# Second cross-attention and feed-forward as one hand-ordered stretch, with softmax inverses and keys and values by way of DRAM

## The chip, the cores and the metric

The kernel runs on one core of one Trainium2 chip. The metric is the device time of one execution in microseconds. A core has five engines that this document speaks of: TensorE (PE in the profile; its weight loads are the row PEld), VectorE (DVE), ScalarE (ACT), GpSimd (POOL) and SyncE (SP), which here only issues DMAs. Each engine works through its own list of instructions in order and waits on semaphores for what others produce. Data moves between DRAM and the on-chip memory (SBUF) by 16 DMA engines; matmul results land in eight banks of PSUM.

## The reference

Two transformer blocks over `x` of shape (8, 512, 256), all in float32. The first block is a self-attention with per-head normed queries and keys, a cross-attention to 64 context tokens, and a gated feed-forward. The second block, cut to what the change touches:

```
cross_in = adaln(x, cond, ...)              # layernorm over 256, then scale and shift per batch
ctx_n    = ln(context)                      # (8, 64, 192)
x = attn(cross_in, ctx_n, ca_wq, ca_wkv, ca_wo, ca_bo) + x
ffn_in = adaln(x, cond, ...)
h = gelu(ffn_in @ ff_w1 + ff_b1)            # 256 -> 1024
x = h @ ff_w2 + ff_b2 + x

attn: q = rope(heads(xq @ wq)); k = rope(heads(ctx @ wk)); v = heads(ctx @ wv)   # 16 heads of 64
      a = softmax(q k^T / 8)                # over the 64 context tokens
      out = (a v) @ wo + bo
```

## The kernel before, in words

All of `x` stays in SBUF as eight tiles of 128 partitions x 4 x 256 (`xs[b]`), and every stage updates it in place. The stages follow one another: block 0 (until about 835 us), block 1's self-attention (the pool `ph4`, until about 1906), its cross-attention (`ph5`, until about 2279) and its feed-forward (`ph6`).

The order of instructions is set in two ways. Block 0 and the self-attention stand under `tc.manual_schedule`, which keeps TensorE, VectorE, ScalarE and POOL in the order in which the program emits them; SP's DMAs are ordered by a planner. The pools `ph5` and `ph6` stand outside it, and the planner orders all engines, starting from `run_blocks`, which places a step some blocks before or after the scores it belongs to.

Self-attention (`slots`) runs over 128 slots: 8 batches x 4 groups of 4 heads x 4 tiles of keys. Each slot makes scores, exponentials, and the products with the values of the slot before. Row sums of the exponentials are made by POOL and VectorE into tiles `sm` (L907, L911) and by TensorE (`sums`). They go by way of DRAM: ScalarE copies them to `den`, a DMA writes them to `den_d` (L929), another reads them back spread over 128 partitions (L935), VectorE takes reciprocals (L939), a DMA writes them to `rec_d` (L941), and two DMAs load them as `rb`, two rows spread over 64 partitions each (L950). POOL multiplies the attention output `oT` by `rb` (L955), and `project_out` makes the output rows of two 128-row tiles, which VectorE adds to `x` (L396). At the end of the stage `cross_values` makes the values of the cross-attention for all batches, eight pairs of heads one after another, and writes them to the DRAM tile `v_d`; the keys `k_d` were written by `keys1` during block 0, with the same layout.

The cross-attention (`batch5`) does for each batch:

- `norm`: layernorm of `x` (L187 to L191, with a power on POOL, L179), eight transposes on TensorE (L366), scale and shift on ScalarE (L367), and the addition of the output bias on POOL (L380).
- `context`: load the keys and values of the batch from `k_d` and `v_d` into one of two buffers, block-diagonally for a pair of heads.
- `outer`: values times output weights for two pairs, so that the weighted sum and the output projection are one matmul per pair (`vw`, L1063).
- `queries(p)`: the query of pair p, then the rope: three VectorE multiplications (L720, L723) and a POOL addition (L724).
- `score`: the scores of two pairs and their exponential on ScalarE (`p`, L1079).
- `sums`: row sums by 16 matmul instructions, VectorE's reciprocal of all 128x512 of them straight from PSUM (L1091), a write to DRAM by four DMAs (L1095), and for each two pairs two loads into `rb`, 64 partitions at a time (L1101), followed by a multiplication of `p` by `rb` on POOL or VectorE in turn (L1104).
- `project_out` with `vw`: the output rows, added to `x`.

The feed-forward makes for each batch four pairs of up-projections with GELU (L1155), prepares the next batch's normed input, projects down and stores the batch. PSUM is shared by `bank_s` (two tiles of two banks, scores), `bank_o` and `bank_d` (one bank each) and `bank_x` (two banks). `bank_x` also takes `bank_d` in turn during block 0, but not after it.

Of the kernel before, what the change touches and what calls it, by code (L numbers as in the profile page):

```python
# [78 lines left out]
def fast_path(ctx: ExitStack, tc: tile.TileContext, a: dict, out: bass.AP):  # L79
# [8 lines left out]
    turns = [0]  # L88
# [10 lines left out]
    def bank_x():  # L99
        if turns:  # L100
            turns[0] += 1
            if turns[0] % 3 == 0:
                return bank_d()
        return psum.tile([P, 512], F32, tag="X", name="ps_X", bufs=2)

# [268 lines left out]

    def normed_T(pool, x, b, eps, am, bm, bufs=2):
        return transposed(pool, normed(pool, b, eps), b, am, bm, bufs)
# [335 lines left out]
    k_d = dram.tile([B, P, NPAIR, T], F32, name="k_d", bufs=1)  # L712
    v_d = dram.tile([B, P, NPAIR, T], F32, name="v_d", bufs=1)
# [23 lines left out]
    def keys1(p):  # L737
        ps = bank_x()
        for k in range(2):
            mm(ps, kv1["w"][:, k, p * P : (p + 1) * P], ctxzT[:, k, :], k == 0, k == 1)  # L740
        q = kv1["pool"].tile([P, N], F32, tag="q", name="q")
        rope_pair(kv1["pool"], ps.rearrange("p (j n) -> p j n", j=B), kv1["rope_c"][:, None, :], kv1["rope_s2"][:, None, :],
                  [P, B, T], q.rearrange("p (j n) -> p j n", j=B))
        nc.sync.dma_start(k_d[:, :, p, :].rearrange("b r t -> r b t"), q.rearrange("p (b t) -> p b t", b=B))
# [56 lines left out]
    turns.clear()  # L801
# [9 lines left out]
    def load_kb(b):  # L811
        for i in range(4):
            r = slice(32 * i, 32 * i + 32)
            nc.sync.dma_start(kvs[b % 2][0][r, :, i % 2, :], k_d[b, r])

    def load_vb(b):
        for e in range(2):
            r = slice(64 * e, 64 * e + 64)
            nc.sync.dma_start(kvs[b % 2][1][r, :, e, :], v_d[b, r])
# [5 lines left out]
    def cross_values(wk, p):  # L825
# [3 lines left out]
        v = wk.tile([P, N], F32, tag="k0", name="v")  # L829
        nc.scalar.copy(v, ps)  # L830
        nc.sync.dma_start(v_d[:, :, p, :].rearrange("b r t -> r b t"), v.rearrange("p (b t) -> p b t", b=B))


    with tc.tile_pool(name="ph4", bufs=2) as wk:
        NG = H // 4
        kb, vb = kv_first()
        steps, mid = {}, {}
# [164 lines left out]
        def slots():  # L1002
            n = B * NG * NT
            for i in range(-2, n + 1):
# [9 lines left out]
                if i == n - 5:  # L1014
                    cross_weights()
            sums, sums_back, inverse, inverse_back, scaled, out_tiles = todo[-1][-1]
# [6 lines left out]
            load_vb(0)  # L1023
            for qp in range(2):
# [5 lines left out]
    w_co, w_cq, rope_s2 = cross["o"], cross["q"], cross["s"]  # L1030


    with tc.tile_pool(name="ph5", bufs=2) as wk:
        kvs.append(tuple(wk.tile([P, NPAIR, 2, T], F32, name=n, bufs=1) for n in ("kb", "vb")))
        for z in kvs[1]:
            nc.gpsimd.memset(z, 0.0)

        w_f1 = load_w("ff_w1", 1)
        w_f2 = load_w("ff_w2", 3)
        blocks = []  # L1040

        def batch5(b):
            s = {}

            def norm():
                s["hT"] = transposed((nk, wk)[b % 2], normed(nk, b, EPS1), b, a1, b1, 1)
                add_row(b, row("cabo"))

            def context():
                s["kb"], s["vb"] = kvs[b % 2]  # L1050
                if b:
                    load_kb(b)
                    load_vb(b)

            def outer(pp):

                if pp == 0:
                    s["vw"] = wk.tile([P, NPAIR, D], F32, tag="vw", name="vw", bufs=3)
                ps = bank_x()
                for i in range(2):  # L1060
                    p = 2 * pp + i
                    mm(ps[:, i * D : (i + 1) * D], s["vb"][:, p, :, :].rearrange("p e k -> p (e k)"), w_co[:, p, :])
                nc.scalar.copy(s["vw"][:, 2 * pp : 2 * pp + 2, :], ps.rearrange("p (i d) -> p i d", i=2))  # L1063

            def queries(p):
                ps = bank_x()
                for k in range(2):
                    mm(ps, w_cq[:, k, p * P : (p + 1) * P], s["hT"][:, k, :], k == 0, k == 1)
                s[p] = q = wk.tile([P, N], F32, tag="q", name="q", bufs=6)
                rope_pair(wk, ps[:, None, :], rope_c[:, None, :], rope_s2[:, None, :], [P, 1, N], q[:, None, :])  # L1070

            def block(pp):
                def score():
                    ps = bank_s()
                    for i in range(2):
                        p = 2 * pp + i
                        mm(ps[:, i, :], s["kb"][:, p, :, :].rearrange("p e k -> p (e k)"), s[p])
                    s["p", pp] = wk.tile([P, 2, N], F32, tag="p", name="p", bufs=8)
                    nc.scalar.activation(s["p", pp], ps, AF.Exp, scale=HD1 ** -0.5)  # L1079

                return Block([score], [])

            def sums():

                d = bank_d()
                for i in range(2):
                    for j in range(4):
                        p = 4 * i + j
                        mm(d[32 * j : 32 * j + 32, :], sel3[:, i, :], s["p", p // 2][:, p % 2, :], i == 0, i == 1)
                rec = wk.tile([P, N], F32, tag="rec", name="rec", bufs=1)  # L1090
                nc.vector.reciprocal(rec, d)  # L1091
                rd = dram.tile([NPAIR, 2, N], F32, tag="rec5", name="rec5")
                for i in range(2):
                    for e in range(2):
                        nc.sync.dma_start(rd[4 * i : 4 * i + 4, e, :],  # L1095
                                          rec.rearrange("(j r) n -> j r n", j=4)[:, 2 * i + e, :])
                check(rec)
                for pp in range(4):
                    rb = wk.tile([P, 2, N], F32, tag="rb", name="rb")
                    for e in range(2):  # L1100
                        nc.sync.dma_start(rb[64 * e : 64 * e + 64, :, :],  # L1101
                                          rd[2 * pp : 2 * pp + 2, e, :][None].to_broadcast([64, 2, N]))
                    eng = (nc.gpsimd, nc.vector)[pp % 2]
                    eng.tensor_tensor(s["p", pp], s["p", pp], rb, ALU.mult)  # L1104

            for pp in range(4):
                bl = block(pp)
                if pp == 0:
                    bl.before += [(5, norm), (4, context)]
                bl.before.append((1, lambda pp=pp: outer(pp)))  # L1110
                bl.before += [(2, lambda pp=pp: queries(2 * pp)), (2, lambda pp=pp: queries(2 * pp + 1))]
                blocks.append(bl)
            bl.after.append((0, sums))
            for qp in range(2):
                bl.after.append((2 + qp, lambda qp=qp: project_out(qp, lambda k: s["p", k // 2][:, k % 2, :], s["vw"], 8,
                                                                  add_to(b))))

        for b in range(B):
            batch5(b)
# [907 lines left out]
```

## Time and profile before

| | us |
|---|---|
| three timed runs, median (range) | 2523.02 (2521.21 to 2523.74) |
| the profiled run: its time | 2522.38 |
| its span, first to last instruction | 2520.5 |

Busy time by stage, in us, from the profiled run:

| stage | length | TensorE | VectorE | ScalarE | POOL | granted TensorE clock | DMA share |
|---|---|---|---|---|---|---|---|
| block 0 (0 to 835) | 835 | 804.7 | 387.7 | 398.0 | 242.8 | 0.98 | 0.12 |
| self-attention of block 1 (to 1906) | 1071 | 1048.7 | 441.4 | 354.6 | 435.6 | 0.99 | 0.08 |
| cross-attention (to 2279) | 373 | 349.0 | 236.1 | 62.8 | 153.1 | 0.99 | 0.24 |
| feed-forward (to the end) | 241.5 | 234.6 | 30.0 | 56.0 | 19.5 | 1.00 | 0.05 |

How to read it: an engine's busy share is an average over the stage; what a stage costs is decided by the engine that others wait for, and by the waits that stand on that engine. The granted clock is the share of full speed at which TensorE was allowed to run. The DMA share is the mean over the 16 DMA engines, so 0.125 can be all of them an eighth of the time or two of them all of the time. Lines of the profile that give a start, a length and in square brackets an idle time name after the arrow what ended that idle time. A float32 matmul shows as two instructions.

### The profile page before, as it was taken

The page shows a single profiled execution, that of the slowest core. Times are in us where ns is not written, and L with a number is a line of the kernel's source. Part 1 is how long each engine was busy: PE and PEld are TensorE (multiplying, and loading weights), DVE is VectorE, ACT ScalarE, POOL GpSimd, SP SyncE. Part 2 cuts the span into 40 slices and gives each one's busy share as a digit, 9 for nine tenths or more (in the row PEclk, how much of TensorE's full clock was granted, in tenths as well). Part 3 has the DMA queues.
Part 4 walks back from the last instruction along what each step waited for, and adds up shares of the span by engine and source line. Part 5 has one row for each costly group of instructions (what it writes and reads, how often), then busy time and mean ns, then how long its engine had stood idle before and what let it go on. Part 6 is the DMA issues. An engine that isn't in the chain of part 4 may idle for free.

```text
span 2520.5 us, 27970 instructions
## 1 busy us (share of the span) xinstructions
PE 2437.0 (97%) x10938; PEld 1152.9 (46%) x10938; DVE 1095.1 (43%) x2039; ACT 871.3 (35%) x1099; POOL 850.9 (34%) x521
## 2 busy tenths in 40 slices
PE   8999999999999899999999999999989999999999
PEld 3333443443445533434343434343435456556665
DVE  4555435435435334343444434445326765652000
ACT  3555546545542133242424243333232111112221
POOL 3453222322300035353535353536324434431000
PEclk9999999999999999999999999999999999999999
DMA  5130000000002000000000000000131321320000
GB/s 180 35 95 9 16 17 10 16 11 12 12 11 88 0 4 28 18 18 18 19 18 18 18 18 18 18 18 18 51 92 40 79 49 42 76 68 9 17 17 26
DMA packets 91084, 83.76 MB, mean 33 GB/s; under 512 B 51104, under 2 KB 67424, under 8 KB 90936
## 3 DMA queue, kind: packets, MB, share of 16 engines
q1 hardware_dynamic: 90388, 81.34, 11.0%
q8 instruction: 88, 1.44, 0.2%
q10 hardware_dynamic: 556, 0.55, 0.1%
q14 instruction: 52, 0.43, 0.1%
HBM read 72.09 MB, written 9.77 MB: 32 GB/s over the span
## 4 chain that ended last, share of the span: by engine, by line
PE 87%; DVE 4%; DMA 3%; issue 2%; POOL 2%; ACT 2%; SPq 0%; DVEq 0%; POOLq 0%; ACTq 0%
PE ps_X L107 42%; PE ps_S L107 22%; PE ps_D L107 11%; PE ps_O L107 9%; PE ps_X L366 1%; DMA rb<-rec_d 1%; DVE t L723 1%; ACT p L505 1%; POOL q L724 1%; DMA rb<-rec 1%; DVE t L720 1%; DVE st L187 1%; PE ps_X L485 0%; POOL p L1104 0%; PE ps_X L527 0%
## 5 line engine op out<-in xcount | busy, mean ns | idle before, releaser
L107 PE MATMUL ps_S<-q,k 32*128 32x512 f32 (+1 forms) x3072 | 432.5, 628 | 7.0 <-ACT p L505 3.4
L892 ACT ACTIVATE p<-ps_S 128x1024 f32<-128x1024 f32 x256 | 248.4, 1022 | 526.6 <-PE ps_S L107 519.1
L505 ACT ACTIVATE p<-ps_S 128x1024 f32<-128x1024 f32 x256 | 248.2, 1022 | 259.7 <-PE ps_S L107 258.8
L107 PEld LDWEIGHTS ps_S<-q,k 32*128 32x128 f32 (+1 forms) x3072 | 160.6, 185 | 245.7 <-issue 136.4
L871 DVE TENSOR_TENSOR t<-ps_X,rope_c 128x512 f32<-128x512 f32 x126 | 87.1, 691 | 341.0 <-PE ps_X L107 341.0
L911 DVE TENSOR_TENSOR sm<-sm,p 128x1024 f32<-128x1024 f32 x128 | 192.3, 1546 | 55.6 <-ACT p L892 54.3
L396 DVE TENSOR_TENSOR x<-ps_X,x 128x512 f32<-128x512 f32 x48 | 33.2, 692 | 342.6 <-PE ps_X L107 342.6
L874 POOL TENSOR_TENSOR q<-t 128x512 f32<-128x512 f32 x32 | 40.7, 1273 | 384.2 <-DVE t L872 384.2
L107 PE MATMUL ps_X<-hT,w 128*128 128x512 f32 x344 | 160.6, 601 | 1.6 <-DVE t L678 1.1
L907 POOL TENSOR_TENSOR sm<-p 128x1024 f32<-128x1024 f32 x64 | 149.2, 2353 | 32.5 <-ACT p L892 32.5
L724 POOL TENSOR_TENSOR q<-t,t 128x512 f32<-128x512 f32 x72 | 97.2, 1353 | 159.0 <-DVE t L723 151.3
L107 PE MATMUL ps_O<-p,h 128*32 128x512 f32 x1024 | 138.1, 612 | 0.5 <-ACT oT L518 0.5
L107 PE MATMUL ps_O<-p,v 128*64 128x512 f32 x512 | 138.0, 617 | 0.0
L107 PE MATMUL ps_D<-p,v 128*64 128x512 f32 x512 | 131.6, 592 | 1.1 <-ACT p L892 1.1
L179 POOL TENSOR_TENSOR rstd<-rstd,mhalf 128x4 f32<-128x4 f32 x49 | 49.6, 1015 | 241.4 <-DVE rstd L178 239.3
L107 PE MATMUL ps_X<-vw,p 128*128 128x256 f32 x512 | 119.2, 389 | 10.9 <-DVE p L1104 9.8
L107 PE MATMUL ps_X<-w_sa_wo,oT 128*128 128x256 f32 x512 | 118.0, 389 | 11.2 <-DVE oT L955 6.4
L380 POOL TENSOR_TENSOR x<-x,rows 128x1024 f32<-128x1024 f32 x24 | 56.5, 2354 | 196.9 <-DVE z L191 195.4
L107 PE MATMUL ps_X<-hT,w_sa_wq 128*128 128x512 f32 x256 | 115.9, 595 | 4.2 <-ACT hT L367 4.2
L107 PE MATMUL ps_X<-w_sa_wv,hT 128*128 128x512 f32 x256 | 118.0, 604 | 0.0
L107 PE MATMUL ps_S<-hT,w_ff_w 128*128 128x512 f32 x256 | 117.9, 604 | 0.1
L107 PE MATMUL ps_X<-hT,w_ca_wq 128*128 128x512 f32 x256 | 117.3, 598 | 0.7 <-DVE t L723 0.7
(219 smaller groups left out, 3546.4 us busy)
## 6 DMA issues: line engine op xcount, KB each, us to landing
rb<-rec SPq DMA_DIRECT2D x80, 256.0 KB
rb<-rec_d SPq DMA_DIRECT2D x62, 256.0 KB
x<-in_x_dram SPq DMA_DIRECT2D x8, 512.0 KB
out_dram<-x SPq DMA_DIRECT2D x8, 512.0 KB
bc<-modd SPq DMA_DIRECT2D x8, 384.0 KB
gate<-modd SPq DMA_DIRECT2D x16, 128.0 KB
k_d<-q SPq DMA_DIRECT2D x8, 256.0 KB
v_d<-v SPq DMA_DIRECT2D x8, 256.0 KB
```

The costliest lines, as they stand in the source:

```text
L107: nc.tensor.matmul(o, lhsT, rhs, start=start, stop=stop)
L179: nc.gpsimd.tensor_tensor(r[:, :n], r[:, :n], mhalf[:, :n], ALU.pow)
L187: nc.vector.bn_stats(st[:, t, :], src[:, t, :])
L380: nc.gpsimd.tensor_tensor(xs[b], xs[b], r[:, None, :].to_broadcast([P, NT, D]), ALU.add)
L396: nc.vector.tensor_tensor(x, ps, x, ALU.add)
L505: nc.scalar.activation(pr[u], pss[u], AF.Exp, scale=HD0 ** -0.5)
L724: nc.gpsimd.tensor_tensor(dst, t1, t2, ALU.add)
L871: nc.vector.tensor_tensor(c, ps, rope_c, ALU.mult)
L874: nc.gpsimd.tensor_tensor(r[0], ec, os, ALU.subtract)
L892: nc.scalar.activation(pr, pss[u], AF.Exp, scale=HD1 ** -0.5)
L907: nc.gpsimd.tensor_tensor(sm, s["p", g, 0, u], s["p", g, 1, u], ALU.add)
L911: nc.vector.tensor_tensor(s["sm", g, u], s["sm", g, u], s["p", g, t, u], ALU.add)
```

## The change

- The cross-attention and the feed-forward become one pool (`ph5`) in one `manual_schedule`, in the order in which `cross()` and `feed_forward()` emit their steps. A batch of the cross-attention is eight steps of a pair of heads. The queries run three pairs ahead of the scores. The inverses, multiplications and output tiles of a batch stand within the next batch's steps; those of the last batch stand within the feed-forward.
- The row sums go to DRAM first (four writes, `den5`), come back spread over 128 partitions, VectorE takes reciprocals of 64 columns, one DMA writes them (`rec5`), and each pair's `rb` is loaded by one DMA as two rows spread over 64 partitions each. POOL and VectorE multiply one pair each in turn.
- `k_d` and `v_d` are laid out by pairs, so that what `keys1` and `cross_values` write is contiguous in each partition; the reads follow.
- The norm and bias addition of batch 0 are emitted in self-attention's slot 123 and its transposes before the last output tiles; values are copied to tiles of two names in turn.
- `bank_x` takes `bank_d` and `bank_o` in turn as well during the new stretch.
- A batch is stored in two halves; the hidden layer has one buffer.

```
-    k_d = dram.tile([B, P, NPAIR, T], F32, name="k_d", bufs=1)
-    v_d = dram.tile([B, P, NPAIR, T], F32, name="v_d", bufs=1)
+    k_d = dram.tile([P, NPAIR, B, T], F32, name="k_d", bufs=1)
+    v_d = dram.tile([P, NPAIR, B, T], F32, name="v_d", bufs=1)
...
-        nc.sync.dma_start(k_d[:, :, p, :].rearrange("b r t -> r b t"), q.rearrange("p (b t) -> p b t", b=B))
+        nc.sync.dma_start(k_d[:, p], q.rearrange("p (b t) -> p b t", b=B))
...
-            nc.sync.dma_start(kvs[b % 2][0][r, :, i % 2, :], k_d[b, r])
+            nc.sync.dma_start(kvs[b % 2][0][r, :, i % 2, :], k_d[r, :, b, :])
...
-        v = wk.tile([P, N], F32, tag="k0", name="v")
+        v = wk.tile([P, N], F32, tag=f"k{p % 2}", name="v")
         nc.scalar.copy(v, ps)
-        nc.sync.dma_start(v_d[:, :, p, :].rearrange("b r t -> r b t"), v.rearrange("p (b t) -> p b t", b=B))
+        nc.sync.dma_start(v_d[:, p], v.rearrange("p (b t) -> p b t", b=B))
...
                 if i == n - 5:
                     cross_weights()
+                    first_rows.append(normed(nk, 0, EPS1))
+                    add_row(0, row("cabo"))
...
             scaled(NG - 1, [nc.gpsimd, nc.vector])
             load_vb(0)
+            first_rows.append(transposed(nk, first_rows[0], 0, a1, b1, 1))
             for qp in range(2):
                 out_tiles(qp)
...
+    extra.extend([bank_d, bank_o])
     with tc.tile_pool(name="ph5", bufs=2) as wk:
...
+        def sums(b):
+            s = ss[b]
+            d = bank_x()
...
+            den = wk.tile([P, N], F32, tag="den", name="den", bufs=1)
+            nc.scalar.copy(den, d)
+            dd = dram.tile([NPAIR, 2, N], F32, tag="den5", name="den5")
+            for i in range(2):
+                for e in range(2):
+                    nc.sync.dma_start(dd[4 * i : 4 * i + 4, e, :], den.rearrange("(j r) n -> j r n", j=4)[:, 2 * i + e, :])
+            s["rec"] = rec = wk.tile([P, H * N // P], F32, tag="rec", name="rec", bufs=1)
+            nc.sync.dma_start(rec, flat(dd))
+
+        def inverse(b):
+            s = ss[b]
+            rec = s["rec"]
+            nc.vector.reciprocal(rec, rec)
+            rd = dram.tile([NPAIR, 2, N], F32, tag="rec5", name="rec5")
+            nc.sync.dma_start(flat(rd), rec)
+            check(rec)
+            s["rd"] = rd
+
+        def scaled(b):
+            s = ss[b]
+            for p in range(NPAIR):
+                rb = wk.tile([P, N], F32, tag="rb", name="rb", bufs=4)
+                nc.sync.dma_start(rb, s["rd"][p, :, None, :].to_broadcast([2, 64, N]))
+                pr = s["p", p // 2][:, p % 2, :]
+                (nc.gpsimd, nc.vector)[p % 2].tensor_tensor(pr, pr, rb, ALU.mult)
+
+        def out_tile(b, t, lhsT, w):
+            s = ss[b]
+            if t % 2 == 0:
+                s["ps"] = bank_x()
+            project_tile(s["ps"], t % 2, lhsT, w, 8, t)
+            if t % 2:
+                add_to(b)(t // 2, s["ps"].rearrange("p (j d) -> p j d", j=2))
...
+        def cross():
+            LEAD = 3
+            for n in range(LEAD):
+                queries(n)
+                if n == 0:
+                    rows_(1)
+            for z in kvs[1]:
+                nc.gpsimd.memset(z, 0.0)
+            for b in range(B):
+                for j in range(NPAIR):
+                    if j % 2 == 0:
+                        score(b, j // 2)
+                    if j == 6 and b:
+                        cross_out(b - 1, 2)
+                    queries(NPAIR * b + j + LEAD)
+                    if j < 2:
+                        outer(b, 2 * j)
+                        outer(b, 2 * j + 1)
+                    if b:
+                        if j == 1:
+                            inverse(b - 1)
+                        if j == 3:
+                            scaled(b - 1)
+                        if j in (4, 5, 7):
+                            cross_out(b - 1, j - 4)
+                    if j == 2 and b + 1 < B:
+                        load_kb(b + 1)
+                        load_vb(b + 1)
+                    if j == 4:
+                        turn(b + 1)
+                    if j == 5:
+                        rows_(b + 2)
+                    if j == 7:
+                        sums(b)
+
+        def feed_forward():
+            good = None
+            for b in range(B):
+                for ff in range(4):
+                    up(b, ff)
+                    if b == 0 and ff == 1:
+                        inverse(B - 1)
+                    if b == 0 and ff == 3:
+                        scaled(B - 1)
+                if b == 0:
+                    for t in range(4):
+                        cross_out(B - 1, t)
+                turn(B + b + 1)
+                for t in range(4):
+                    down(b, t)
+                    if t == 1:
+                        rows_(B + b + 2)
...
+        with tc.manual_schedule(engines={ENG.PE, ENG.DVE, ENG.Activation, ENG.Pool}):
+            cross()
+            return feed_forward()
```

`rows_` is the layernorm and bias addition of a batch, `turn` its transposes with scale and shift, `cross_out(b, t)` the output tile t of the cross-attention, `up` and `down` the two halves of the feed-forward.

## The prediction

> **What bounds the kernel now.** I read the page's first part, then busy time by stage, then the chain and TensorE's waits in the last two stages, and last the queue rows and DMA share around the loads called rb.
>
> ```profile
> PE 2437.0 (97%) x10938; PEld 1152.9 (46%) x10938; DVE 1095.1 (43%) x2039; ACT 871.3 (35%) x1099; POOL 850.9 (34%) x521
> ...
> 1906.00:2279.00 373.00, 348.97 (x1217) 201.54 (x1215) 236.11 (x354) 62.77 (x80) 153.07 (x98) 0.99 0.24 59
> 2279.00:2520.50 241.50, 234.59 (x836) 149.20 (x834) 29.99 (x66) 56.00 (x81) 19.50 (x10) 1.00 0.05 18
> ```
>
> TensorE (first number after each length) is the bound, also in the second cross-attention (1906 to 2279) and the feed-forward. All that a better order could win there is its idle time, 24 and 7 us. The waits from 1855 on say where it is:
>
> ```profile
> PE ps_X L107 <- DVE p L1104: 9.8, 5, 2.8
> PE ps_S L107 <- POOL q L724: 6.8, 13, 1.5
> PE ps_X L107 <- DVE oT L955: 6.4, 1, 6.4
> PE ps_X L107 <- POOL oT L955: 4.9, 1, 4.9
> ```
>
> Most of it is output tiles waiting for products with rb, the softmax inverses that come back from DRAM. So the question is how fast rb comes back. Self-attention loads it as two rows, each spread over 64 partitions (L950); SP issues two such loads and POOL multiplies when each lands:
>
> ```profile
> 1838.18 1.13 SPq L950 DMA_DIRECT2D rb<-rec_d  x2
> ...
> 1845.80 1.27 POOL L955 TENSOR_TENSOR oT<-oT,rb 128x512 f32<-128x512 f32 x1 [9.89 <-DMA rb<-rec_d]
> 1851.09 1.28 POOL L955 TENSOR_TENSOR oT<-oT,rb 128x512 f32<-128x512 f32 x1 [4.01 <-DMA rb<-rec_d]
> ```
>
> The first lands 7.6 us after the issue, the second 5.3 us behind it; the next pair (issue 1854.57, use 1862.11 and 1867.38) repeats that: 7.5 and 5.3. The last two columns here are DMA share and GB/s, during self-attention's rb (outer size 2), the first cross-attention's (L634, outer size 8) and today's second cross-attention's (L1101, outer size 64):
>
> ```profile
> 1644.00:1653.00 9.00, 9.00 (x28) 3.44 (x24) 4.33 (x5) 3.11 (x4) 0.00 (x0) 1.00 0.13 51
> 243.00:244.00 1.00, 1.00 (x12) 0.29 (x12) 0.69 (x1) 0.65 (x1) 1.00 (x1) 1.00 0.48 184
> 2056.00:2060.00 4.00, 4.00 (x12) 2.18 (x12) 1.03 (x2) 1.02 (x2) 2.38 (x3) 1.00 1.02 233
> ```
>
> 0.13, 0.48 and 1.02 are two, eight and sixteen of 16 DMA engines: the outer size of the source sets how many work. The new `scaled` loads each rb as `[2, 64, N]`, self-attention's form, and eight of them per batch, where L1101 has `[64, 2, N]`. In self-attention 11 us of loads hide in 30 us of scores. That is the heart of the forecast.
>
> One rule of the Trainium skill speaks against the change. "DMA: Bandwidth & Descriptors", Rules for kernel authors, "Use all 16 engines", says that a leading zero-stride or short outer dimension of c copies confines a DMA to at most c engines; the shares above bear it out. Its Specifications give about 27 GiB/s per engine; an estimate from that is 4.5 us for 256 KB on two engines against the 5.3 measured, 6 us less per batch and a total near 2756 us. The row decides.
>
> **A steady batch** (T is the end of the previous batch's `sums` on TensorE). Prices from rows: `queries` or one `score` 1.72 us (8 instructions in 3.43), `outer` 0.86, an output tile 3.46 (32 instructions in 6.92), eight transposes 0.88, `sums` 2.0 (8 instructions in 1.00). A batch is 40.8 us of TensorE work; today's takes 46.3 (92.6 us between the like rows at 2077.92 and 2170.51, two batches).
> - `den`: ScalarE copy done at T+0.75; four writes at 0.55 issue each (L1095), landing 1.7 after the last issue (as from L929 to L935 at 1658.76); the read back takes 1.7 (L935 at 1867.56 to reciprocal at 1869.28): T+5.9, not on the path, since
> - `inverse` stands on VectorE behind the rope of the query made in step 1: TensorE ends that at T+7.0, rope 2.1 (0.69 and 1.39), reciprocal of 64 columns about 0.55 (0.24 for 16, 0.34 for 32): T+9.65. Write to rb issue 1.47 (L941 to L950): T+11.15.
> - Eight rb of 256 KB: first usable 7.58 after issue, then 5.28 each (four buffers keep the queue fed): the last at T+55.7. VectorE's product 0.69 and a semaphore: T+56.6. TensorE has reached that operand of `cross_out` tile 0 at T+21 and, in program order, waits. Behind it stand `turn`, three `queries`, a `score` and three output tiles; VectorE and POOL stand in `scaled` all that time, the last query's rope behind them.
> - After it: last matmul pair 0.43, transposes and the wait for ScalarE's hT 1.7 (2279.10 to 2281.14, less a 0.35 bank wait), three output tiles 10.4, three `queries` 5.15, `score` 1.72, `sums` 2.0, gaps 0.5: 21.9.
> - Clock: after the 6.36 us wait at 1892 TensorE ran at 0.50 for 4.85 us more, which loses 2.4:
>
> ```profile
> 1892.00:1897.00 5.00, 4.55 (x11) 3.66 (x12) 0.39 (x1) 0.00 (x0) 0.00 (x0) 0.50 0.26 60
> ```
>
> Together 56.6+21.9+2.4 = 80.9 us per batch. "TensorE: Matmul & The Clock Gate", Part 1, gives a free-running window of 3.4 us at half rate, an estimate of 1.7 lost per restart, 6 us less in all; but the trace also dropped to 0.50 at 2078.5 after a gap of only 1.98 us, so I keep 2.4.
>
> **Ahead of it.** Batch 0's norm and row addition now stand in self-attention's POOL and VectorE order behind `scaled(1)`, which ends at 1852.37. POOL's power (1.02), VectorE's four scalings (1.4) and POOL's addition (2.35) come before the last `sm` additions (today 1852.34), so these and `sums` behind them slide about 5 us; none if there were room, but POOL has none there. Against that, v_d's writes go from 256-byte pieces to 2 KB ones, and the last rb (today used 17.6 us after issue, 12.9 in the undisturbed pair) should take about 14.5. Net on the last output tiles: 1905.85+1.9 = 1907.8; ends -4.7 (no slide, 12.9) and +5.
>
> Batch 0: `rows_(1)` stands ahead of query 1's rope: statistics and aggregates 1.9, rstd 0.2, power 1.0, scalings 1.4, rope 2.1, POOL's row addition and query sum until 10.4 us after query 0; TensorE is free at 3.4. Stall 7.0, clock 2.4, work 32.9, gaps 0.5: 42.8; no gain is possible below the 33 of work.
>
> **Behind it.** Batches 1 to 7 take 7x80.9, less three queries (5.2) in the last: 561.1. In the feed-forward `up` of batch 0 covers 14.5 us; rb issues at T+7.95 (VectorE is free) and the last product is at T+53.4; then 10.8 of tiles, 2.4 of clock, 0.9, `down` 13.84, and seven batches of which six at today's 29.3 and one at 28.5: with a tail of 5.3 (today 6.3; the last store is half as large) 291 us in all. `hid` in one buffer costs nothing: `down` stands before the next `up` on TensorE.
>
> **At nothing.** VectorE's reciprocal falls from 3.36 to 0.55 and its range check from 1.3: VectorE is 63% busy and then waits anyway. More PSUM banks: the 0.1 to 0.2 us gaps they could close are in "gaps". Key and value reads have 256-byte pieces on the SBUF side before and after; they take 2 us on each engine and free buffers let them go early; at worst they sit in rb's way for 1.4 us per batch. Writing k_d by pairs may shorten a 4.0 us wait at 176.5 by 1.5 (0 to 5.7 with the clock).
>
> **Sum.** 1907.8+42.8+561.1+291-1.5 = 2801.2 of span; the profiled run has 1.9 outside its span and stands 0.6 below the median of 2523.0: 2804 us.
>
> **Rivals.**
> - rb spreads over 16 engines as in L1101 (1.25 us each, first after 3.65): the last product is at T+24.3, the stall 3.3 and a batch 47.3, a total near 2535. If it also came before TensorE asks (T+21), no stall is left and it ends at 2505: faster. It decides at about 1.1 us per load. For: nothing but that the SBUF side has 128 partitions; against: L950 has that too, and runs at 0.13. On eight engines, as L634, a load takes 1.4 (184 GB/s) and the case is the same. Faster 0.04, same 0.02, slower 0.03.
> - VectorE becomes a second hold-up: after `scaled` it owes two ropes, an addition and a norm with POOL's power, and the last `score` needs the first rope (margin 4 us: T+59.8 against T+64). If that fails, up to 8 us more in each of seven batches: 2860. Chance 0.08.
>
> **The numbers.** Two-engine loads as summed: 0.83. Per batch the issue of rb could be 1.7 earlier, the restart cost 0.7 less or 1 more, gaps 1 more, other loads 1.4 in the way: -24 to +27 over eight, and -7 to +5 at the seams: 2773 to 2836. I stretch to 2765 to 2850, towards the second rival; some 0.2 lies outside. Faster, within 0.2% (about what this kernel's runs can tell from no change) and slower: 0.04, 0.02, 0.94.
>
> **What would show it.** Right: in each of batches 1 to 7 some 42 us with a DMA share near 0.13 and 50 GB/s; TensorE waiting for DVE and POOL p, these for DMA rb; products 10.6 us apart on each of the two; granted clock 0.5 in the second half of each batch; a POOL wait for norm before `sm` at 1852. Wrong: a share near 1 during rb, or a period other than about 81 us per batch.

## The result, and the profile after

| | us |
|---|---|
| the changed kernel, median of four runs (range) | 2832.54 (2828.67 to 2835.52) |
| the kernel before beside it, median of four runs (range) | 2522.49 (2521.21 to 2523.74) |
| ratio, with its 95% interval | 1.1228 (1.1209 to 1.1248) |
| span of the profiled run of the changed kernel | 2826.9 |

The changed kernel is 310 us, or 12.3%, slower. The forecast was 2804 us with a range of 2765 to 2850. The time lies in the range, 28.5 us above the number.

The first lines of the page of the changed kernel, busy time by engine, and below them its stages (length, then busy time of TensorE, weight loads, VectorE, ScalarE and POOL, then granted TensorE clock, DMA share and GB/s). The third and fourth stage are now the batches of the cross-attention until the last `sums`, and what follows.

```profile
PE 2486.8 (88%) x10938; PEld 1172.7 (41%) x10938; DVE 1053.7 (37%) x2055; ACT 876.9 (31%) x1107; POOL 849.1 (30%) x537
```

```profile
835.00:1906.00 1071.00, 1049.73 (x4826) 454.47 (x4826) 429.29 (x633) 356.34 (x451) 432.91 (x275) 0.99 0.07 23
1906.00:2507.00 601.00, 370.34 (x1143) 206.26 (x1142) 199.80 (x372) 67.89 (x87) 146.72 (x112) 0.77 0.10 34
2507.00:2826.90 319.90, 260.88 (x917) 165.74 (x915) 39.29 (x110) 55.30 (x80) 26.85 (x17) 0.94 0.06 21
```

Up to 1906 nothing has moved that matters. From there the cross-attention takes 601 us with TensorE busy for 370, where before it took 373 with 349. TensorE's instructions are the same in number (10938); it stands idle for 231 us. The waits of TensorE from 1855 on (total, how often, longest) name what it stands for:

```profile
PE ps_X L109 <- POOL p L1121: 62.1, 15, 4.7
PE ps_X L109 <- DVE p L1121: 56.1, 16, 3.9
PE ps_D L109 <- POOL p L1121: 32.7, 8, 4.7
PE ps_O L109 <- POOL p L1121: 31.9, 8, 4.7
PE ps_D L109 <- DVE p L1121: 28.4, 8, 3.9
PE ps_O L109 <- DVE p L1121: 28.4, 8, 3.9
PE ps_S L109 <- ACT hid L1143: 25.0, 32, 0.9
PE ps_S L109 <- POOL q L723: 18.0, 11, 5.9
```

The first six rows are one thing in three banks: 240 us of waiting for the products with `rb`, four products on POOL and four on VectorE in each of eight batches. What these two wait for, in the page's groups (busy time and mean of one, then the idle time before it):

```profile
L1121 DVE TENSOR_TENSOR p<-p,rb 128x512 f32<-128x512 f32 x32 | 22.2, 692 | 307.7 <-DMA rb<-rec 307.7
L1121 POOL TENSOR_TENSOR p<-p,rb 128x512 f32<-128x512 f32 x32 | 40.3, 1261 | 251.8 <-DMA rb<-rec 251.8
```

And the like of the queue's rows shown before, in the first of these batches: the issue of eight loads on SP, and the products on POOL and VectorE with their idle time.

```profile
1967.93 30.30 SPq L1119 DMA_DIRECT2D rb<-rec  x8
1975.80 1.26 POOL L1121 TENSOR_TENSOR p<-p,rb 128x512 f32<-128x512 f32 x1 [1.74 <-DMA rb<-rec]
1981.00 0.69 DVE L1121 TENSOR_TENSOR p<-p,rb 128x512 f32<-128x512 f32 x1 [8.36 <-DMA rb<-rec]
1986.35 1.26 POOL L1121 TENSOR_TENSOR p<-p,rb 128x512 f32<-128x512 f32 x1 [9.29 <-DMA rb<-rec]
...
2012.63 0.69 DVE L1121 TENSOR_TENSOR p<-p,rb 128x512 f32<-128x512 f32 x1 [9.84 <-DMA rb<-rec]
```

The first product comes 7.9 us after the issue, each next one 5.2 to 5.4 us later, 10.55 us apart on each engine. During such a stretch the stage view has, in its last two columns, the share and rate that self-attention's `rb` had:

```profile
1970.00:2013.00 43.00, 11.76 (x23) 4.42 (x21) 5.03 (x8) 1.02 (x1) 7.57 (x6) 0.60 0.13 48
2051.00:2093.00 42.00, 10.90 (x20) 4.37 (x20) 4.04 (x6) 1.02 (x1) 6.91 (x6) 0.58 0.13 48
```

That is the share of two of the 16 DMA engines. It isn't all of them for an eighth of the time: counted from the packets' starts and lengths in the trace, two packets are under way for 91% of the stretch from 2057 to 2091, and more for 8%. The rows of `sums` on TensorE's timeline start at 1951.06, 2033.80, 2114.55, 2194.13, 2274.82, 2354.54, 2434.97 and 2509.16: seven batches in 558.1 us, 79.7 each on average (82.7 the first, 74.2 the last, which has three queries less).

### The profile page after: what moved, and what is told of

It reads as the page before. It is cut to its first block, busy times and chain, and to the rows that moved or that the text cites. A ratio compares the mean times of both kernels' runs of the same rounds, so it can differ in the third digit from the quotient of the medians.

```text
span 2826.9 us, 28034 instructions
## 1 busy us (share of the span) xinstructions
PE 2486.8 (88%) x10938; PEld 1172.7 (41%) x10938; DVE 1053.7 (37%) x2055; ACT 876.9 (31%) x1107; POOL 849.1 (30%) x537
## 4 chain that ended last, share of the span: by engine, by line
PE 78%; DMA 13%; DVE 2%; ACT 2%; POOL 1%; SPq 1%; issue 1%; DVEq 0%; POOLq 0%; ACTq 0%
PE ps_X L109 32%; PE ps_S L109 20%; PE ps_D L109 13%; PE ps_O L109 11%; DMA rb<-rec 11%; SPq L1119 1%; DMA rb<-rec_d 1%; PE ps_X L368 1%; ACT hid L1143 1%; ACT p L504 1%; DMA rec<-rec 0%; DVE t L722 0%; PE ps_X L484 0%; PE ps_X L526 0%; ACT hT L369 0%
## 5 line engine op out<-in xcount | busy, mean ns | idle before, releaser
L892 ACT ACTIVATE p<-ps_S 128x1024 f32<-128x1024 f32 x256 | 248.2, 1022 | 528.6 <-PE ps_S L109 520.1
L109 PE MATMUL ps_X<-vw,p 128*128 128x256 f32 x192 | 68.1, 494 | 118.2 <-POOL p L1121 62.1
L723 POOL TENSOR_TENSOR q<-t,t 128x512 f32<-128x512 f32 x72 | 91.2, 1267 | 240.3 <-DVE t L722 185.2
L1121 DVE TENSOR_TENSOR p<-p,rb 128x512 f32<-128x512 f32 x32 | 22.2, 692 | 307.7 <-DMA rb<-rec 307.7
L1121 POOL TENSOR_TENSOR p<-p,rb 128x512 f32<-128x512 f32 x32 | 40.3, 1261 | 251.8 <-DMA rb<-rec 251.8
L109 PEld LDWEIGHTS ps_X<-w_sa_wo,oT 128*128 128x128 f32 x512 | 97.6, 193 | 35.9 <-issue 11.4
```

The source lines that it names most:

```text
L109: nc.tensor.matmul(o, lhsT, rhs, start=start, stop=stop)
L723: nc.gpsimd.tensor_tensor(dst, t1, t2, ALU.add)
L892: nc.scalar.activation(pr, pss[u], AF.Exp, scale=HD1 ** -0.5)
L1121: (nc.gpsimd, nc.vector)[p % 2].tensor_tensor(pr, pr, rb, ALU.mult)
```

## The experiments

All medians stand beside runs of the kernel before on the same chip (2521 to 2524 us), and each ratio is to those. Theory A is the forecast's: the form of the `rb` loads sets the number of DMA engines. Theory F came from the seventh row of the waits above. Two 512-column halves of a `ps_S` tile are written by TensorE and read by two GELUs; in the changed order the first GELU is emitted between the two products, and the second product then waits for it.

**1. Spread the loads.** Each `rb` of the changed kernel by two DMAs of one row to 64 partitions.

```
-                nc.sync.dma_start(rb, s["rd"][p, :, None, :].to_broadcast([2, 64, N]))
+                for e in range(2):
+                    nc.sync.dma_start(rb[64 * e : 64 * e + 64, :], s["rd"][p, e : e + 1, :].to_broadcast([64, N]))
```

> The changed kernel with each rb loaded by two DMAs, one row spread over 64 partitions each, in place of one DMA of two rows. Theory A (the two-row form puts the load on two DMA engines): DMA share near 1 while rb loads, a batch of the cross-attention about 47 us instead of 80, the wait in the feed-forward's first batch gone; seven batches give back 32 to 34 us each and the feed-forward 33, so about 2563 us (2545 to 2585). Rival V (VectorE and POOL, which stand in the products, or the hand-written order itself hold the batch): the period stays above 70 us and the total above 2750.

Measured: 2594.46 us (2588.99 to 2599.30), ratio 1.0269 (1.0246 to 1.0293). So 238 of the 310 us are the form of these loads, or their number, which doubles here (runs 5 and 6 tell the two apart). The time is 31 us above the number expected, beyond its range, and the expected share near 1 didn't come either. The stage view over the loads of one batch:

```profile
2079.00:2095.00 16.00, 9.17 (x23) 3.71 (x21) 5.97 (x9) 1.02 (x1) 8.43 (x6) 0.88 0.38 127
```

In steps of half a microsecond the share is 0.44 to 0.68 from 2078.5 to 2083.5, nothing from 2084 to 2086, and 0.38 to 0.80 in a second burst from 2086.5 to 2091. That fits eight loads into the four buffers, at the pace at which SP issues them (16 in 12.75 us), and eight more when these come free. The waits of TensorE from 1840 on in this run are led by the row of theory F; the six rows of `p` have come down from 240 us to under 40:

```profile
PE ps_S L109 <- ACT hid L1144: 25.0, 32, 0.9
PE ps_S L109 <- POOL q L723: 18.0, 11, 5.9
PE ps_X L109 <- POOL p L1122: 12.3, 11, 2.4
PE ps_D L109 <- POOL p L1122: 9.3, 8, 2.1
PE ps_O L109 <- POOL p L1122: 8.7, 8, 2.5
```

**2. Both products, then both GELUs.** Only `up` of the changed kernel is edited.

```
             for i in range(2):
                 f = 2 * ff + i
                 for k in range(2):
                     mm(ps[:, i, :], w_f1[:, k, f * P : (f + 1) * P], ...)
+            for i in range(2):
+                f = 2 * ff + i
                 nc.scalar.activation(s["hid"][:, f, :], ps[:, i, :], AF.Gelu, ...)
```

> The changed kernel with the two GELUs of a pair issued after both matmuls of the pair, not between them. Theory F (TensorE may write the second half of a PSUM tile only after ScalarE has read the first half, 0.78 us at 32 places, which the planner's order had covered): these waits go, a feed-forward batch falls from 32.6 to about 29.3 us, the total by 25 to 2807 us (2800 to 2815). Rival H (the hidden layer's single buffer or the halved stores make the feed-forward longer): no change, 2832 us.

Measured: 2801.06 us (2800.15 to 2804.44), ratio 1.1099 (1.1077 to 1.1122): 31.5 us less than the changed kernel. The same groups of TensorE's work from the view by line, first of the changed kernel (from 2500 on), then of this run (from 2400 on):

```profile
L109 PE MATMUL ps_S<-hT,w_ff_w 128*128 128x512 f32 x256 | 119.8, 606 | 25.0 <-ACT hid L1143 25.0
```

```profile
L109 PE MATMUL ps_S<-hT,w_ff_w 128*128 128x512 f32 x256 | 111.3, 592 | 0.0
```

The 25.0 us of waits are gone, and 8.5 us of busy time with them (the mean of one matmul falls from 606 to 592 ns). That is over all eight batches, and the first doesn't count: there TensorE waits for `rb` that much longer, and uses the last product at 2564.57 in the changed kernel and at 2564.67 here. The other seven go from 32.6 to 28.4 us each. Theory F holds, and rival H falls: the order of four instructions costs 29 us by these traces, 31.5 between the medians.

**3. Both edits.**

> Both edits. Theory A with F: the two gains add, 2563 - 25 = 2538 us (2520 to 2560), still a little slower than before: what is left is the wait in front of the cross-attention's first scores and some 3 us of waiting per batch. Rival V: above 2725 us.

Measured: 2562.75 us (2560.75 to 2566.73), ratio 1.0156 (1.0135 to 1.0178). The two gains add up (238 and 32), and 25 us above the expectation remain, 3 us beyond its range. They lie in the cross-attention: its batches take 50.7 to 51.2 us here. SP's own rows in a steady batch show where the time may go, which run 7 tests: 16 loads take 12.7 us to issue, with four buffers, after the second half of the value loads.

```profile
2065.62 0.33 SPq L1111 DMA_DIRECT2D rec<-rec  x1
2066.00 0.58 SPq L818 DMA_DIRECT2D vb<-v_d  x1
2067.66 12.66 SPq L1120 DMA_DIRECT2D rb<-rec  x16
```

**4. The form alone, on the kernel before.** There the planner orders the engines, and the loads were `[64, 2, N]`; here the same tile is loaded by as many DMAs of as many bytes, in the other order of dimensions. The rival O holds that it was the hand-written order, in which TensorE can't put other work into a wait, that cost the time.

```
-                        nc.sync.dma_start(rb[64 * e : 64 * e + 64, :, :],
-                                          rd[2 * pp : 2 * pp + 2, e, :][None].to_broadcast([64, 2, N]))
+                        nc.sync.dma_start(rb[:, e, :], rd[2 * pp + e, :, None, :].to_broadcast([2, 64, N]))
```

> The kernel before, its order left to the planner, with each rb tile loaded as two DMAs of two rows spread over 64 partitions each instead of two DMAs of 64 partitions with two rows each. Same bytes, same number of DMAs. Theory A: the loads of a batch take 42 us on two engines; TensorE asks for the last product about 30 us after the row sums and gets it after about 54: some 24 us per batch, 2650 to 2760 us, DMA share 0.13 while they load. Rival O (it is the hand-written order that costs; the planner's order hides slow loads): within 40 us of before, 2520 to 2560 us.

Measured: 2772.16 us (2769.97 to 2781.57), ratio 1.0993 (1.0965 to 1.1021), 12 us above the range expected. The form alone costs 249 us, under the planner's order too, so rival O falls. A stretch of 25 us in a batch of this run, in the stage view's columns:

```profile
2127.00:2152.00 25.00, 3.75 (x8) 2.52 (x8) 3.98 (x5) 0.00 (x0) 5.39 (x3) 0.58 0.17 57
```

TensorE is busy for 3.75 of them. The share is 0.13 where no value or key loads run beside `rb` (2132 to 2138). TensorE's waits from 1900 on also include 54.4 us for `DVE t L723`, the rope of a query: this rope stands behind the product in VectorE's order, and the product waits for `rb`.

**5 and 6. Four and sixteen rows outermost, one DMA for each tile.** To tell "two DMAs" from "more rows outermost", each row of inverses is written k times to DRAM, and a tile is loaded by one DMA from 2k rows. Shown for k = 2; for k = 8 it is `[16, 8, N]`.

```
-            rd = dram.tile([NPAIR, 2, N], F32, tag="rec5", name="rec5")
-            nc.sync.dma_start(flat(rd), rec)
+            rd = dram.tile([NPAIR, 2, 2, N], F32, tag="rec5", name="rec5")
+            for c in range(2):
+                nc.sync.dma_start(rd[:, :, c, :].rearrange("p e (a b) -> (p e) a b", b=H * N // P), rec)
...
-                nc.sync.dma_start(rb, s["rd"][p, :, None, :].to_broadcast([2, 64, N]))
+                nc.sync.dma_start(rb, s["rd"][p].rearrange("e c n -> (e c) n")[:, None, :].to_broadcast([4, 32, N]))
```

> The changed kernel; each row of reciprocals is written twice to DRAM, and a pair's load becomes one DMA of [4, 32, N] in place of one of [2, 64, N]: same number of loads, same bytes written to SBUF, four outer rows. Theory A in its sharp form (a load gets as many of the 16 DMA engines as its access has outermost rows): a load takes 2.64 us in place of 5.28, the last product of a batch comes 21 us sooner, in seven batches and at the feed-forward's start: 2832 - 8 x 21 = 2664 us (2640 to 2690). Rival P (what mattered was that a pair was loaded by two DMAs): 2825 to 2840.

> The same with eight copies: one DMA of [16, 8, N] for each pair, eight small writes in place of one. Theory A in its sharp form: all 16 engines, as with the two DMAs of [64, N] (2594 us), with 8 issues of 0.6 us in place of 16 and 7 more writes of 0.33 us: 2580 us (2560 to 2600). Rival P: 2825 to 2840, or slower by the added writes.

Measured: 2670.43 us (2670.26 to 2670.75) with four rows, ratio 1.0586 (1.0564 to 1.0608); 2597.76 us (2594.52 to 2598.28) with sixteen, ratio 1.0294 (1.0272 to 1.0316). Both are in their ranges, 6 and 18 us above their numbers. Rival P, which held that it was the number of DMAs, falls in both. Stretches of `rb` loads in the first and in the second of these runs, stage view:

```profile
2028.00:2052.00 24.00, 12.79 (x26) 4.98 (x24) 6.22 (x9) 1.02 (x1) 7.53 (x6) 0.71 0.26 94
```

```profile
2078.00:2091.00 13.00, 9.82 (x21) 5.06 (x20) 4.46 (x6) 1.02 (x1) 6.32 (x5) 0.67 0.59 170
```

And TensorE's timeline with four rows, one pair of matmuls for each product:

```profile
2041.54 1.22 PE L109 MATMUL ps_O<-vw,p 128*128 128x256 f32 x2 [2.05 <-POOL p L1122]
2043.54 1.22 PE L109 MATMUL ps_O<-vw,p 128*128 128x256 f32 x2 [0.78 <-DVE p L1122]
2046.82 1.22 PE L109 MATMUL ps_O<-vw,p 128*128 128x256 f32 x2 [2.05 <-POOL p L1122]
```

Two products come every 5.28 us, so a load takes 2.64 us: half of what it took with two rows outermost, at twice the share (0.26 against 0.13). With sixteen the share reaches 0.97 to 1.04 in single steps of half a microsecond and falls to 0.17 between two bursts. The eight writes took SP 5.04 us to issue, 0.63 each, where 0.33 had been expected; how much of the 18 us is theirs wasn't tried.

**7. Eight loads into one tile.** To run 3: the inverses of a batch go into one tile of eight pairs (the hidden tile's place, unused at that time) by eight DMAs of `[64, 2, N]`, and `inverse` is emitted a step earlier. The last batch uses eight query tiles instead, two DMAs each.

```
+            rb = wk.tile([P, 8, N], F32, tag="hid", name="rb", bufs=1)
+            for pp in range(4):
+                for e in range(2):
+                    nc.sync.dma_start(rb[64 * e : 64 * e + 64, 2 * pp : 2 * pp + 2, :],
+                                      s["rd"][2 * pp : 2 * pp + 2, e, :][None].to_broadcast([64, 2, N]))
...
-                        if j == 1:
+                        if j == 0:
                             inverse(b - 1)
```

> The changed kernel with both earlier edits (spread loads of the reciprocals, both GELUs after both products of a pair), which took 2562.75 us with a batch pitch of 50.8 us, plus: the reciprocals of a batch go into one tile of eight heads' pairs (the feed-forward's hidden tile, not in use yet) by 8 DMAs of [64, 2, N] in place of 16 of [64, 1, N] into four rotating buffers, and they are issued a step earlier. Theory I (what is left of the batch pitch is SyncE's issue, 16 x 0.6 us plus the wait of the second four pairs for a free buffer): eight issues without a buffer wait take about 5 us instead of 12.6, the last product comes 4 to 7 us earlier, seven batches: 2525 us (2510 to 2540). Rival W (what is left is the transfer itself, 4 MB written per batch over 16 engines): the bytes are the same, the pitch stays above 49 us: 2550 to 2565.

Measured: 2533.77 us (2532.67 to 2536.53), ratio 1.0044 (1.0029 to 1.0059). The eight loads issue in 5.14 us, a batch takes 46.5 us, and 29 us are won. That is 9 us above theory I's number, within its range, and clear of rival W's (whose 4 MB are 2 MB: eight tiles of 256 KB). While these loads run, from 2062.5 to 2071.5, the share is 0.87 to 1.16 in steps of half a microsecond. The edit makes two moves at once (fewer loads without buffer waits, and the earlier `inverse`); their shares weren't told apart.

**8. Self-attention's loads too, on the kernel before.** L950 as two DMAs of one row, as in run 1; nothing else.

> The kernel before with only self-attention's reciprocal loads (two rows to 64 partitions each from one DMA with two outer rows) issued as two DMAs of one row over 64 partitions. If the theory of the load's form is right it holds outside the changed part too: the waits of 4.9 and 6.4 us on these tiles at 1880 to 1892 us go, and the half clock after them: 2512 us (2506 to 2519). If these loads are late for another reason (the reciprocal before them, the queue): 2519 to 2528.

Measured: 2505.88 us (2502.60 to 2511.41), ratio 0.9932 (0.9919 to 0.9946): 17 us faster than the kernel before. The output tiles of self-attention, from 835 to 1950, first in the kernel before and then in this run:

```profile
L107 PE MATMUL ps_X<-w_sa_wo,oT 128*128 128x256 f32 x512 | 118.0, 389 | 11.2 <-DVE oT L955 6.4 <-POOL oT L955 4.9
```

```profile
L107 PE MATMUL ps_X<-w_sa_wo,oT 128*128 128x256 f32 x512 | 114.7, 382 | 0.0
```

The two waits are gone, and 3.3 us of busy time with them, which fits the half clock behind the waits.

**9. The same on run 7.**

> The kernel of c1 (2533.8 us) plus only self-attention's reciprocal loads spread (worth 17 us on the kernel before); the three seams stay. If the parts of c2 add up: 2517 us (2511 to 2523), and the seams of c2 are then worth 26 us. If the loads and the seams cover one another: 2525 or more.

Measured: 2508.44 us (2506.12 to 2510.62), ratio 0.9941 (0.9920 to 0.9962), 25 us below run 7 and 3 us below the range expected. Besides the two `oT` waits (6.1 and 4.6 us) the wait of 4.6 us for `ACT p L892`, which the forecast had put down to the norm's place in POOL's order, is gone as well. POOL's timeline near the norm of batch 0, first in run 7 and then in this run:

```profile
1848.04 1.28 POOL L955 TENSOR_TENSOR oT<-oT,rb 128x512 f32<-128x512 f32 x1 [3.99 <-DMA rb<-rec_d]
...
1854.09 4.64 POOL L907 TENSOR_TENSOR sm<-p 128x1024 f32<-128x1024 f32 x2
```

```profile
1836.96 2.52 POOL L957 TENSOR_TENSOR oT<-oT,rb 128x512 f32<-128x512 f32 x2 [5.99 <-DMA rb<-rec_d]
...
1844.42 4.67 POOL L907 TENSOR_TENSOR sm<-p 128x1024 f32<-128x1024 f32 x2
```

With both `rb` there together POOL has multiplied by 1839.5 in place of 1849.3 (2.1 us of this are an earlier issue, at 1833.05 in place of 1835.11), and `sm` is no longer late behind the norm. The slide was partly the loads' doing, which the expectation had not priced. The interval of this ratio overlaps that of run 8: with the loads spread (in run 7's form, issued a step earlier) and the GELUs grouped, the hand-written order takes about as long as the planner's.

**10. The seams.** To run 9: the first four queries ahead of `rows_(1)` (a lead of four, with an eighth query buffer), batch 0's norm four slots earlier, each `turn` ahead of the step's query.

```
                 if i == n - 5:
                     cross_weights()
+                if i == n - 9:
                     first_rows.append(normed(nk, 0, EPS1))
...
-            LEAD = 3
+            LEAD = 4
             for n in range(LEAD):
                 queries(n)
-                if n == 0:
-                    rows_(1)
+            rows_(1)
...
+                    if j == 4:
+                        turn(b + 1)
                     queries(NPAIR * b + j + LEAD)
...
-                    if j == 4:
-                        turn(b + 1)
```

> The kernel of c1 plus the seams mended: the first four queries ahead of the row norm of batch 1, the row norm of batch 0 four slots earlier, self-attention's last reciprocal loads spread over 64 partitions each by two DMAs, each batch's turn ahead of its queries. Theory I and the forecast's seam terms (5 us of slide, 7 us of first stall, both with the throttle's lower clock after them, plus two waits of 4.9 and 6.4 us at 1880 to 1892 that the kernel before has as well): 20 to 28 us below c1, that is 2500 us (2485 to 2520), under the kernel before. Rival R (each seam only uncovers the next releaser in line): less than 8 us below c1.

Measured: 2490.69 us (2489.27 to 2491.72), ratio 0.9869 (0.9854 to 0.9884): 33 us, 1.3%, faster than the kernel before, 43 us below run 7, where 20 to 28 had been expected, and 18 below run 9. Rival R falls. What each of the three moves gives wasn't told apart. The page's first line of this run, and the first rows of its waits from 1840 on:

```profile
PE 2420.0 (97%) x10938; PEld 1157.0 (46%) x10938; DVE 1068.8 (43%) x2055; ACT 872.0 (35%) x1107; POOL 864.0 (35%) x537
```

```profile
PE ps_X L109 <- POOL p L1139: 8.8, 12, 1.3
PE ps_D L109 <- POOL p L1139: 7.2, 7, 3.6
PE ps_X L109 <- ACT hT L369: 4.5, 5, 0.9
PE ps_O L109 <- DVE t L722: 3.8, 1, 3.8
```

The 18 us of waits for `POOL q` have left the list, and a batch takes 44.9 us. TensorE still waits about 18 us for POOL's products. In the batch at 2035.67 these are no longer held up by `rb`: POOL makes its four back to back in 6.28 us. Here the products of the two engines fall into the same time, and take longer: a median of 1.71 us on POOL and 1.10 us on VectorE, against 1.26 and 0.69 us in the changed kernel, where they stand apart.

**11. Keys and values by pairs, alone.** The kernel before with only the change's layout of `k_d` and `v_d` and the second name for the value tiles.

> The kernel before with only the change's third part: keys and values in DRAM by pairs of heads (one write of [128, 512] rows for each pair, read back as before). The forecast's term: minus 1.5 us; 2521 us (2515 to 2524). Rival: the layout costs something at the reads or at the seam into the cross-attention, 2526 or more.

Measured: 2522.37 us (2519.76 to 2526.66), ratio 0.9999 (0.9990 to 1.0008). No difference of 2.5 us or more in either direction; the 1.5 us of the forecast can't be told from none. The wait that it was to shorten went from 4.0 to 3.2 us.

## Why the prediction was right, point by point, and where its sizes were off

**The heart, the form of the loads: right, and shown.** Runs 1, 4, 5 and 6 change little but the form, on two orders of instructions, and move the time by 162 to 249 us. Two and four rows outermost go with shares of 0.13 and 0.26 and load times of 5.28 and 2.64 us. The forecast's price of 5.28 us each is met in the row, as are 7.58 to the first use (7.87), 10.6 between products (10.55), 42 us at a share of 0.13 in each batch, and the last product of the feed-forward's start at T+53.4 (its end is at 2564.5, T is 2511.1).

**The sum, term by term.** Ends by the trace, against the forecast's terms:

| term | forecast | trace |
|---|---|---|
| last output tiles of self-attention, with k_d's 1.5 | 1906.3 | 1909.2 |
| batch 0 | 42.8 | 43.8 |
| batches 1 to 7 | 561.1 | 558.1 |
| feed-forward part | 291 | 315.8 |
| span | 2801.2 | 2826.9 |

All but the last term hold within 3 us. Inside them errors cancel. `rb` is issued at T+14.9 in the first batch, after a wait of 2.83 us for `POOL q`, and at T+11.4 to T+12.0 in later ones, where 11.15 was worked out (the second half of the value loads stands between the write of the inverses and `rb` on SP, which the forecast had only as a bound of 1.4). So the last product comes to TensorE at T+60.4 in the first batch and at T+56.6 to T+57.4 in later ones, where 56.6 was forecast. What follows takes 22.3 to 23.8 in place of 24.3.

The 2.4 us for the clock in these 24.3 were about right. Three neighbouring stretches after the first batch's last product:

```profile
2013.00:2016.00 3.00, 2.62 (x10) 2.24 (x10) 2.39 (x4) 0.45 (x1) 0.40 (x1) 0.50 0.00 0
2016.00:2019.00 3.00, 2.93 (x10) 1.57 (x9) 0.53 (x1) 1.10 (x2) 0.86 (x1) 0.94 0.00 0
2019.00:2034.00 15.00, 15.00 (x62) 10.66 (x64) 10.00 (x24) 1.02 (x1) 6.81 (x5) 1.00 0.08 19
```

Here the clock is back 3.0 us after the last product, by the clock's record in the trace. In the eight places where TensorE restarts in this way it takes 3.0, 5.2, 3.1, 5.6, 3.1, 6.1, 4.1 and 4.8 us, which at half clock lose 1.5 to 3.0 us, 2.2 on average. The forecast's estimate from "TensorE: Matmul & The Clock Gate", Part 1 (one window of 3.4 us at half rate, 1.7 us lost), is near the three shortest of them and below the mean; the row at 1892 was the better price. Without that loss what follows takes 20.8 us in each of the batches 1 to 6, so it is the forecast's 21.9 for the work that was 1.1 too long.

Some figures of the forecast don't close. Of its waits from 1855 on, the two of 6.4 and 4.9 us stand at 1880 to 1892, ahead of the 24 us that they were to explain; inside these the waits for products are 10.8. The first rival's 47.3 us a batch is 1.1 above its terms (24.3 and 21.9). The range's -24 is 8 x (1.7 + 0.7), which is 19. None of the three moves the forecast's time.

**The step that failed: "`hid` in one buffer costs nothing: `down` stands before the next `up` on TensorE", with six batches "at today's 29.3".** The buffer does cost nothing, but the price of a batch was carried over from a trace in which the planner had ordered `up`. The diff takes that planner away, and the order that the program writes, product, GELU, product, GELU, was not priced. On TensorE's timeline of the changed kernel:

```profile
2626.55 1.88 PE L109 MATMUL ps_S<-hT,w_ff_w 128*128 128x512 f32 x4
2629.20 3.70 PE L109 MATMUL ps_S<-hT,w_ff_w 128*128 128x512 f32 x8 [0.78 <-ACT hid L1143]
2633.68 3.70 PE L109 MATMUL ps_S<-hT,w_ff_w 128*128 128x512 f32 x8 [0.78 <-ACT hid L1143]
...
2659.15 1.88 PE L109 MATMUL ps_S<-hT,w_ff_w 128*128 128x512 f32 x4
```

Four waits of 0.78 us a batch are most of the step from 29.3 to 32.6. They count in the seven batches after the first, with 21.8 of the 24.8 us by which this term is off. In the first batch they fall into time in which TensorE would wait for `rb` anyway, and the last product comes at T+53.4 as forecast; that all 32 waits together make 25.0 is chance. Of the rest, 1.5 us are the range check of the inverses (`within`), where TensorE waits 1.07 us for `DVE top L1155`. Run 2 takes the waits out and lands at 2801, beside the forecast's 2804. Part of that is luck: its batch takes 28.4 us, 0.9 less than the 29.3 that were carried over.

**The first rival, 16 engines, 2535 us.** It didn't come about in the changed kernel. Run 1 gave its loads the outer size of 64 that this rival needs and stayed at 2594, so the rival's price was mis-sized too: by the GELUs (run 3, 32 us) and by 1.25 us for a load, taken from the 512 KB that L1101 loads by two DMAs into half as many tiles. Sixteen smaller loads into four buffers took SP 12.7 us to issue. With both mended, and the inverses a step earlier than in the rival's sum, run 7 took 2534.

**The second rival, VectorE as a second hold-up,** has no row: TensorE's waits for `POOL q` in batches 2 to 7 are single ones of 1.1 us, and these batches are not above the forecast. (Batch 1, with waits of 2.83 and 1.09 us, is 1.8 above.) In run 4, where a rope stands behind a waiting product, something of the kind appears (54.4 us).

**The seams** were as worked out in kind: POOL's row addition of the norm at 1852.29 delays `sm` to 1854.60, TensorE then waits 4.42 us for `ACT p`, and batch 0 stalls on `POOL q` for 0.48 and 5.92 us (7.0 was forecast). At the last output tiles two sizes were off and nearly cancel. The last `rb` is issued 3.1 us later than before (1877.15 against 1874.07), where a slide of 5 was put down. And it is used 18.5 us after its issue, where the new layout of `v_d` was to bring 17.6 down to 14.5; with that layout alone, in run 11, it is 19.3. **k_d's 1.5 us** were neither shown nor excluded (run 11).

## What to carry to other kernels

Look at the outermost dimension of every broadcast load before its bytes: in this kernel the same 256 KB took 5.28 us with two rows outermost and 2.64 with four, and putting the 64 partitions outermost removed 238 of the 310 us. Where a planner's order is replaced by one written out by hand, price each short producer and consumer pair afresh, since figures from the old trace include the interleaving that the planner did. A wait that is hidden behind one stage can be the bound when its form is copied to a stage without cover; the same form also cost the kernel before 17 us at the one place where its cover ended.

## What the runs showed of the hardware that was not expected

- The time of one load halved exactly when its outer rows doubled (5.28 and 2.64 us for 256 KB; 48 and 94 to 100 GB/s): 24.8 GB/s for each of two and of four engines. "DMA: Bandwidth & Descriptors", in the section "Why a DMA increments its semaphore by 16 and not by 1", says that the number of engines is the largest up to 16 that divides the slowest dimension (sizes of 1 aside) of both sides. The shares at 2 and 4 agree with it, and so does the 1.02 of the kernel before with 64 partitions outermost. The rate doesn't go on in proportion: at that 1.02 it was 233 GB/s, some 14 for each of 16 engines.
- A product into one half of a `ps_S` tile waited for ScalarE's read of the other half, 0.78 us each time, though the halves lie in two banks; with both products ahead of both reads no wait was left (run 2). Whether the chip would need this wait wasn't tried; it stands in the program as a semaphore.
- TensorE's clock stays at 0.50 through stalls in which it runs a pair of matmuls every 5 us (from 1978.83 to 2016.38 in the first batch), and is back 3.0 to 6.1 us after dense work begins. Every stay of the clock from 1855.95 to the feed-forward's end is a multiple of 3.41 us long (37.55 and 40.96 in the stalls), so what a restart costs depends on where in this grid it falls.
- Products of VectorE and POOL that fall into the same time took longer than apart: 1.10 and 1.71 us against 0.69 and 1.26 (medians, run 10 and the changed kernel). What slows them wasn't tried.
